# A neighbour mask turned by VectorE instead of TensorE, and the order of the steps around it

## The chip, the cores and the metric

The kernel runs on one core of a Trainium2 chip. The metric is device time in microseconds (us): the median over runs of one whole execution. Below, PE is TensorE's matmul side and PEld its weight loads, DVE is VectorE, ACT is ScalarE, POOL is GpSimd, and SP is the engine on whose queue most DMAs are issued.

## The reference

Two graph layers run over 128 graphs of 128 nodes with 256 channels, in float32. The change lies in the message part of the first layer:

```python
def _L0_gnn_ref(x, mask, w_se, b_se, conv1_w, ..., w_msg, b_msg, w_ih, b_ih, w_hh, b_hh):
    ...                                   # x_conv: two convolutions over the nodes, the second with 17 taps
    s = x @ w_se.T + b_se                 # 3 channels a node
    sq = jnp.sum(s * s, axis=-1)
    dist = sq[:, :, None] + sq[:, None, :] - 2.0 * jnp.einsum('bnd,bmd->bnm', s, s)
    A = jnp.exp(-dist) * mask
    msg = jax.nn.relu(x @ w_msg.T + b_msg)
    x_nmp = jnp.einsum('bnm,bmd->bnd', A, msg)
    x_in = jnp.concatenate([x_conv, x_nmp], axis=-1)
    ...                                   # a GRU cell of x_in and x
    return (1.0 - z) * nn_ + z * x

h = jnp.maximum(_layernorm(x, axis=-1), 0.0)
x = x + _L0_gnn_ref(h, adj, ...)
...                                       # layer 1: five small graph convolutions on the first 25 nodes
```

`adj` is [128, 128, 128] and holds zeros and ones.

## The kernel before

Graphs are worked on in groups of four (`GB`), so there are 32 groups `q`. The program is written as generators, and a small planner decides the order in which their steps are put on the engines' queues.

**The planner.** `Order.run` (lines 183 to 204) takes a set of lanes. A lane holds a list of generators and a weight. Every `yield cost, wait` ends a step: the planner's clock goes on by `cost`, and the generator isn't due again until `wait` later. The planner takes the lane with the least cost done for its weight whose next generator is due. The order is fixed when the program is built; on the chip each engine runs its queue in that order and waits on semaphores.

**The stages.** Lines 1129 to 1150 run two batches, each of a preparing stage and a product stage. `stage_a` (389) normalises 16 groups, transposes them, applies the first convolution and goes to frequencies. `stage_b` (502) does the second convolution as products by frequency: at each of 40 steps it loads weights (`load_w`, 509, `wf`, issued three steps ahead), adds them on POOL (`add`, 517), multiplies on PE (`product`, 523) into PSUM tiles `pa` and `pb`, and evicts with ACT and DVE (556 to 559). A lane called `beside` runs next to all of that: first the weights of the taps, then `early(q)` (662) for q from 0 to 31. After the two batches the gates (`stage_c`, 713), the rest of `beside` and layer 1 share PE (1149).

**The messages of a group.** `early(q)` takes the tiles that were loaded a group ahead, has `load_n(q + 1)` (571) issued on SP's queue, and runs `neighbours` (608). `load_n` loads `hT`, the normalised group with channels on partitions, and `ad`, the mask of four graphs with the target node on partitions. `neighbours` then goes through these steps, with the planner's cost and wait in brackets:

- an embedding on PE into `pse` (614), four scaled copies `ef` on ACT (618) and their product `lr` on DVE (621) [0.5, 0.0];
- twice a message: eight passes on PE into `pm` (630), the bias on DVE (633) and relu on ACT (635) [1.75, 0.0 each];
- the distances: for each of the four graphs a matmul with a 32-row slice of `lr` into the first half of a PSUM tile `pd` (643); for each a transpose of its mask through the identity into the second half (645); for each the exponential on ACT into `aT` (647) and the multiply with the transposed mask, read from PSUM, on DVE (648) [0.9, 3.0];
- twice `px`, the messages times `aT` (656), and its eviction on DVE (658) [0.9, 0.0 each].

PSUM tiles with the tag "tmp" come from one pool of five banks, `ptmp` (218), which all lanes share in turn; the four `pd` tiles take four of them. The SBUF tiles of `neighbours` come from the pool `fr` with one buffer each, those of `load_n` from `io` with two.

These few lines set the step that is changed:

```python
639        pds = [ptmp.tile([P, 2, N], FP, tag="tmp", name=f"pd{q}_{j}") for j in range(GB)]
643            nc.tensor.matmul(pds[j][:, 0], lr[rows, 0], lr[rows, 1], start=True, stop=True)
645            nc.tensor.transpose(pds[j][:, 1], ad[:, j], ident)
647            nc.scalar.activation(aT[:, j], pds[j][:, 0], AF.Exp)
648            nc.vector.tensor_mul(aT[:, j], aT[:, j], pds[j][:, 1])
```

`convolved` (689) has a turn by DVE already: `nc.vector.transpose` (705) turns each 32x32 block of a 128x512 tile by itself. Layer 1 has a load of short runs already, of the first 25 columns of the mask (`prepare`, 964).

Of the kernel before, what the change touches and what calls it, by code (L numbers as in the profile page):

```python
# [9 lines left out]
FP = mybir.dt.float32  # L10
AF = mybir.ActivationFunctionType
# [4 lines left out]
B, N, D = 128, 128, 256  # L16
# [3 lines left out]
P = 128  # L20
GB = 4
# [20 lines left out]
WIDE = 32  # L42
# [165 lines left out]
def kernel(ctx: ExitStack, tc: tile.TileContext, x, adj, consts, vecs, w_se, conv1_w,  # L208
                    conv2_w, w_msg, b_msg, w_ih, w_hh, W1, W2, b2, fusion_w, out):
    nc = tc.nc  # L210
# [7 lines left out]
    ptmp = ctx.enter_context(tc.tile_pool(name="ptmp", bufs=5, space=PSUM))  # L218
# [14 lines left out]
    def c(name):  # L233
        a, b = CAT[name]
        return cst[:, a:b]
# [5 lines left out]
    ident = c("ident")  # L241
# [127 lines left out]
    LATE, XA, MOM = {}, {}, {}  # L369
# [201 lines left out]
    def load_n(q):  # L571
        hT = LATE["io"].tile([P, 2, 512], FP, tag="hT", name=f"hT{q}")
        nc.sync.dma_start(out=hT, in_=hTd[q])
        ad = LATE["io"].tile([P, GB, N], FP, tag="adj", name=f"adj{q}")
        nc.sync.dma_start(out=ad, in_=adj[q * GB:(q + 1) * GB].rearrange("b n m -> n b m"))
        return hT, ad

    SUMS = {}
# [29 lines left out]
    def neighbours(q, hT, ad, xm):  # L608


        pse = ptmp.tile([P, 512], FP, tag="tmp", name=f"pse{q}")
        for k in range(2):
            for j in range(GB):
                nc.tensor.matmul(pse[j * WIDE:(j + 1) * WIDE, :N], wse9[:, k],  # L614
                                 hT[:, k, j * N:(j + 1) * N], start=(k == 0), stop=(k == 1))
        ef = LATE["fr"].tile([P, 4, N], FP, tag="ef", name=f"ef{q}")
        for i in range(4):
            nc.scalar.activation(ef[:, i], pse[:, :N], AF.Identity, scale=emb[:, i:i + 1],
                                 bias=embb[:, i:i + 1])
        lr = LATE["fr"].tile([P, 2, N], FP, tag="lr", name=f"lr{q}")  # L620
        nc.vector.tensor_tensor(lr, ef[:, 0::2], ef[:, 1::2], ALU.mult)
        yield 0.5, 0.0

        msgs = []
        for h in range(2):
            pm = ptmp.tile([P, 2, D], FP, tag="tmp", name=f"pm{q}_{h}")
            for i in range(2):
                j = 2 * h + i
                for k in range(2):
                    nc.tensor.matmul(pm[:, i], hT[:, k, j * N:(j + 1) * N], LATE["wmsg"][:, k],  # L630
                                     start=(k == 0), stop=(k == 1))
            msg = LATE["fr"].tile([P, 2, D], FP, tag=f"msg{h}", name=f"msg{q}_{h}")
            nc.vector.tensor_tensor(
                msg, pm, LATE["bmsg"][:, None, :].to_broadcast([P, 2, D]), ALU.add)
            nc.scalar.activation(msg, msg, AF.Relu)
            msgs.append(msg)
            yield 1.75, 0.0

        pds = [ptmp.tile([P, 2, N], FP, tag="tmp", name=f"pd{q}_{j}") for j in range(GB)]
        aT = LATE["fr"].tile([P, GB, N], FP, tag="aT", name=f"aT{q}")  # L640
        for j in range(GB):
            rows = slice(j * WIDE, (j + 1) * WIDE)
            nc.tensor.matmul(pds[j][:, 0], lr[rows, 0], lr[rows, 1], start=True, stop=True)
        for j in range(GB):
            nc.tensor.transpose(pds[j][:, 1], ad[:, j], ident)
        for j in range(GB):
            nc.scalar.activation(aT[:, j], pds[j][:, 0], AF.Exp)
            nc.vector.tensor_mul(aT[:, j], aT[:, j], pds[j][:, 1])
        yield 0.9, 3.0


        for h in range(2):
            px = ptmp.tile([P, 2, 2, N], FP, tag="tmp", name=f"px{q}_{h}")
            for i in range(2):
                for dc in range(2):
                    nc.tensor.matmul(px[:, dc, i], msgs[h][:, i, dc * P:(dc + 1) * P],  # L656
                                     aT[:, 2 * h + i], start=True, stop=True)
            nc.vector.tensor_copy(xm[:, :, h * 256:(h + 1) * 256],
                                  px.rearrange("p d i n -> p d (i n)"))
            yield 0.9, 0.0  # L660

    def early(q):

        while q not in A_DONE:
            yield 0.0, 0.5
        if q not in EN:
            EN[q] = load_n(q)
            yield 0.0, 6.0
        hT, ad = EN.pop(q)
        if q + 1 < NQ and q + 1 in A_DONE:  # L670
            EN[q + 1] = load_n(q + 1)
        xm = LATE["fr"].tile([P, 2, 512], FP, tag="xnmp", name=f"xnmp{q}", bufs=2)
        yield from neighbours(q, hT, ad, xm)
        nc.gpsimd.dma_start(out=xmd[q], in_=xm)
        E_DONE.add(q)
# [516 lines left out]
```

## Time and profile before

| What | Value |
|---|---|
| median of three runs | 2033.72 us (2030.26 to 2035.86) |
| the profiled run's own time | 2034.12 us |
| span of that run | 2032.3 us |
| TensorE clock granted over the span | 0.994 |
| DMA packets, bytes | 190266, 281.91 MB |
| mask transposes on PE (L645) | 128, 21.0 us busy |
| mask multiplies on DVE (L648) | 128, 28.0 us busy |
| loads of the mask for the messages (L575) | 32 of 256 KB |
| first and last weight load of L645 | 179.1 and 807.5 us |

In rows of instructions the columns are the line, engine, operation, output and inputs, shape and count, then busy us, the mean ns of one, and the idle time of the engine just before them with what ended it. In the order of time a row begins with the start and the length of a run of like instructions, both in us. A busy PE includes the time in which pipelined matmuls drain, so two rows of PE can overlap.

### The profile page before, as it was taken

How to read it: one execution, taken by the hardware profiler on the slowest of the kernel's cores; microseconds unless marked ns; L12 is line 12 of the kernel's file. 1: busy time of each engine (PE TensorE's matmuls, PEld its weight loads, DVE VectorE, ACT ScalarE, POOL GpSimd, SP SyncE). 2: the span in 40 equal slices, each digit the busy share in tenths (PEclk: the TensorE clock that was granted, in tenths of full speed). 3: DMA queues.
4: the chain of work that ended last, by engine and by line, in shares of the span. 5: the costliest groups of instructions: out<-in, count | busy, mean ns of one | idle time of the engine just before them, and what ended most of it. 6: DMA issues, size and time to landing. Idle time of an engine off the chain costs nothing.

```text
span 2032.3 us, 34053 instructions
## 1 busy us (share of the span) xinstructions
PE 1989.3 (98%) x12852; PEld 1653.7 (81%) x12852; DVE 1285.2 (63%) x2807; ACT 683.8 (34%) x1547; POOL 741.2 (36%) x898
## 2 busy tenths in 40 slices
PE   7998999999999999999999999999999999999998
PEld 5666888889888888778788878878888888878875
DVE  6774445785433566766775775677577757766643
ACT  4663222454222344232322322232233322232233
POOL 3542666332655022532333233224323323332330
PEclk9999999999999999999999999999999999999999
DMA  9987879744877633432322322322232323232121
GB/s 214 297 266 226 269 255 285 222 145 161 269 257 254 188 115 89 147 90 68 105 73 84 96 83 73 97 83 80 82 108 68 90 84 93 79 100 84 37 82 53
DMA packets 190266, 281.91 MB, mean 139 GB/s; under 512 B 23745, under 2 KB 143494, under 8 KB 190102
## 3 DMA queue, kind: packets, MB, share of 16 engines
q1 hardware_dynamic: 157062, 185.46, 31.5%
q0 software_dynamic: 32656, 93.98, 14.2%
q8 instruction: 102, 1.67, 0.4%
q14 instruction: 62, 0.51, 0.1%
q10 hardware_dynamic: 384, 0.28, 0.1%
HBM read 187.34 MB, written 92.27 MB: 138 GB/s over the span
## 4 chain that ended last, share of the span: by engine, by line
PE 90%; DVE 3%; issue 2%; DMA 2%; POOL 2%; ACT 1%; SPq 0%; POOLq 0%; DVEq 0%; ACTq 0%
PE p L741 41%; PE pa L526 7%; PE pm L630 5%; PE ph L1049 5%; PE pz L1058 5%; PE pc L421 4%; PE pb L526 3%; PE px L656 3%; PE pf L432 3%; PE pi L698 3%; PE po L887 1%; PE ph L410 1%; PE py L1032 1%; PE pw L474 1%; PE pse L614 1%
## 5 line engine op out<-in xcount | busy, mean ns | idle before, releaser
L867 POOL TENSOR_TENSOR hTc<-hTc,r 128x512 f32<-128x512 f32 x64 | 88.7, 1385 | 255.8 <-ACT r L864 255.8
L526 PE MATMUL pa<-wf,X 128*128 128x256 f32 x640 | 152.2, 381 | 0.0
L558 DVE SCALAR_TENSOR_TENSOR y<-pa,kk 128x512 f32<-128x512 f32 x78 | 53.8, 690 | 151.2 <-ACT kk L557 151.1
L896 POOL DMA_DIRECT2D out<-xt x128 | 72.0, 569 | 175.1 <-DVE xt L893 172.0
L741 PE MATMUL p<-th,wrz 128*128 128x256 f32 x512 | 134.6, 385 | 0.0
L741 PE MATMUL p<-tc,wrz 128*128 128x256 f32 x512 | 131.5, 379 | 0.0
L741 PE MATMUL p<-tm,wrz 128*128 128x256 f32 x512 | 131.4, 379 | 0.0
L526 PEld LDWEIGHTS pa<-wf,X 128*128 128x128 f32 x640 | 118.2, 190 | 16.1 <-issue 2.0
L421 PE MATMUL pc<-c1w,hTa 128*128 128x256 f32 x512 | 122.3, 386 | 1.9 <-DVE X L438 1.7
L630 PE MATMUL pm<-wmsg,hT 128*128 128x256 f32 x512 | 123.4, 387 | 0.0
L1051 ACT ACTIVATE hh<-ph,vec 128x96 f32<-128x96 f32 (+3 forms) x160 | 63.8, 401 | 140.8 <-PE ph L1049 131.7
L1049 PE MATMUL ph<-yz,w 128*128 128x96 f32 (+3 forms) x640 | 109.7, 325 | 1.0 <-issue 1.0
L421 PEld LDWEIGHTS pc<-c1w,hTa 128*128 128x128 f32 x512 | 95.0, 192 | 18.9 <-DVE h L424 4.8
L741 PEld LDWEIGHTS p<-th,wrz 128*128 128x128 f32 x512 | 94.6, 190 | 19.1 <-issue 7.4
L630 PEld LDWEIGHTS pm<-wmsg,hT 128*128 128x128 f32 x512 | 97.0, 193 | 16.1 <-issue 1.6
L710 ACT ACTIVATE xc<-xc,t_bn 128x256 f32<-128x256 f32 x128 | 58.0, 500 | 149.2 <-DVE xc L707 149.2
L741 PEld LDWEIGHTS p<-tm,wrz 128*128 128x128 f32 x512 | 97.4, 190 | 13.1
L1058 PE MATMUL pz<-hh,w 128*128 128x96 f32 (+3 forms) x640 | 107.3, 322 | 0.0
L1049 PEld LDWEIGHTS ph<-yz,w 128*128 128x128 f32 x640 | 88.4, 194 | 21.3 <-issue 14.5
L741 PEld LDWEIGHTS p<-tc,wrz 128*128 128x128 f32 x512 | 95.0, 190 | 11.6
L1058 PEld LDWEIGHTS pz<-hh,w 128*128 128x128 f32 x640 | 86.6, 191 | 17.7
L741 PE MATMUL p<-hTc,wrz 128*128 128x256 f32 x384 | 98.9, 380 | 0.0
(200 smaller groups left out, 4579.5 us busy)
## 6 DMA issues: line engine op xcount, KB each, us to landing
wf<-wfd SPq DMA_DIRECT2D x160, 256.0 KB
wfd<-ws POOLq DMA_DIRECT2D x64, 320.0 KB, 9.2
yd<-y POOLq DMA_DIRECT2D x80, 256.0 KB, 4.1
yt<-yd SPq DMA_DIRECT2D x64, 320.0 KB
w<-in_W SPq DMA_DIRECT2D x40, 512.0 KB
xa<-in_x SPq DMA_DIRECT2D x128, 128.0 KB
hTd<-hTa POOLq DMA_DIRECT2D x32, 512.0 KB, 6.5
hT<-hTd SPq DMA_DIRECT2D x32, 512.0 KB
```

The costliest lines, as they stand in the source:

```text
L421: nc.tensor.matmul(pc[:, i], hT[:, k, (2 * h + i) * N:(2 * h + i + 1) * N], c1w[:, k], start=(k == 0), stop=(k == 1))
L432: nc.tensor.matmul(pf[:, i, :F * NB], h1[:, 2 * h + i, k * P:(k + 1) * P], fwd, start=True, stop=True)
L526: nc.tensor.matmul(ps, xk(k), WF[f][:, k, s], start=(k == 0), stop=(k == 1))
L630: nc.tensor.matmul(pm[:, i], hT[:, k, j * N:(j + 1) * N], LATE["wmsg"][:, k], start=(k == 0), stop=(k == 1))
L656: nc.tensor.matmul(px[:, dc, i], msgs[h][:, i, dc * P:(dc + 1) * P], aT[:, 2 * h + i], start=True, stop=True)
L698: nc.tensor.matmul(pi[w * WIDE:(w + 1) * WIDE, :, :, n].rearrange("p k g c -> p g k c"), inv[:F, o:o + WIDE], yt[:, n // 2::2].rearrange(" ...
L741: nc.tensor.matmul(ps[:, m], w[:, i, k, m * P:(m + 1) * P], factor(i, x, t), start=first and j == 0, stop=last and j == len(n) - 1, skip_g ...
L867: nc.gpsimd.tensor_sub(d, d, r[:, dc])
L896: nc.gpsimd.dma_start(out=out[q * GB + j, WIDE:].rearrange("(t n) c -> n t c", n=WIDE), in_=xt[j * WIDE:(j + 1) * WIDE, 1:4])
L1049: nc.tensor.matmul(ph, w1[:, k, m * P:(m + 1) * P], yz[:, k, :, o:o + n], start=(k == 0), stop=(k == 1))
L1051: nc.scalar.activation(hh[:, m], ph, AF.Relu, bias=v("b1", g * 4 + m))
L1058: nc.tensor.matmul(pz, w2[:, g, m, cc * P:(cc + 1) * P], hs[g][:, m], start=(m == 0), stop=(m == 3))
```

## The change

The mask is loaded in blocks: four DMAs a group, one for each 32 columns, put each 32x32 block of a mask where one turn by DVE of the 128x512 tile gives the transposed mask `adT` in SBUF. The runs in memory become 32 elements (128 bytes) long instead of 128. The four transposes on PE are gone, and so is the second half of each `pd`. The turn is the first instruction of `neighbours`. The multiplies read two SBUF tiles, and there are two of 128x256 instead of four of 128x128. The distances move between the first and the second message, and the costs and waits that the steps tell the planner change from (0.5, 0), (1.75, 0), (1.75, 0), (0.9, 3.0) to (0.5, 0), (1.75, 3.0), (0.45, 3.0), (1.75, 0.3); the two of `px` stay.

```diff
     def load_n(q):
...
-        ad = LATE["io"].tile([P, GB, N], FP, tag="adj", name=f"adj{q}")
-        nc.sync.dma_start(out=ad, in_=adj[q * GB:(q + 1) * GB].rearrange("b n m -> n b m"))
+        ad = LATE["io"].tile([P, GB * 4, WIDE], FP, tag="adj", name=f"adj{q}")
+        for w in range(4):
+            nc.sync.dma_start(out=ad[w * WIDE:(w + 1) * WIDE],
+                              in_=adj[q * GB:(q + 1) * GB, :, w * WIDE:(w + 1) * WIDE]
+                              .rearrange("b (k n) m -> n (b k) m", n=WIDE))
...
     def neighbours(q, hT, ad, xm):
+        adT = LATE["fr"].tile([P, GB, N], FP, tag="adT", name=f"adT{q}")
+        nc.vector.transpose(adT.rearrange("p b n -> p (b n)"),
+                            ad.rearrange("p b n -> p (b n)"))
         pse = ptmp.tile([P, 512], FP, tag="tmp", name=f"pse{q}")
...
-        for h in range(2):
+        def message(h):
             pm = ptmp.tile([P, 2, D], FP, tag="tmp", name=f"pm{q}_{h}")
...
-            yield 1.75, 0.0
-        pds = [ptmp.tile([P, 2, N], FP, tag="tmp", name=f"pd{q}_{j}") for j in range(GB)]
+        message(0)
+        yield 1.75, 3.0
+        pds = [ptmp.tile([P, N], FP, tag="tmp", name=f"pd{q}_{j}") for j in range(GB)]
         aT = LATE["fr"].tile([P, GB, N], FP, tag="aT", name=f"aT{q}")
         for j in range(GB):
             rows = slice(j * WIDE, (j + 1) * WIDE)
-            nc.tensor.matmul(pds[j][:, 0], lr[rows, 0], lr[rows, 1], start=True, stop=True)
+            nc.tensor.matmul(pds[j], lr[rows, 0], lr[rows, 1], start=True, stop=True)
         for j in range(GB):
-            nc.tensor.transpose(pds[j][:, 1], ad[:, j], ident)
-        for j in range(GB):
-            nc.scalar.activation(aT[:, j], pds[j][:, 0], AF.Exp)
-            nc.vector.tensor_mul(aT[:, j], aT[:, j], pds[j][:, 1])
-        yield 0.9, 3.0
+            nc.scalar.activation(aT[:, j], pds[j], AF.Exp)
+            if j % 2:
+                nc.vector.tensor_mul(aT[:, j - 1:j + 1], aT[:, j - 1:j + 1], adT[:, j - 1:j + 1])
+        yield 0.45, 3.0
+        message(1)
+        yield 1.75, 0.3
```

## The prediction

> **What bounds the kernel now.** I read the page's busy shares first, then a table of stretches, then the order of instructions around one mask, then who waits for whom.
>
> ```profile
> PE 1989.3 (98%) x12852; PEld 1653.7 (81%) x12852; DVE 1285.2 (63%) x2807; ACT 683.8 (34%) x1547; POOL 741.2 (36%) x898
> ...
> PE 90%; DVE 3%; issue 2%; DMA 2%; POOL 2%; ACT 1%; SPq 0%; POOLq 0%; DVEq 0%; ACTq 0%
> ```
>
> TensorE is busy for 98% of the span and makes 90% of the chain that ended last. A busy PE includes pipelined ends, so the price of an instruction has to come from the distance to the next start, not from its duration.
>
> ```profile
> 280.00:490.00 210.00, 206.37 (x1315) 183.31 (x1314) 141.23 (x351) 86.65 (x207) 90.93 (x110) 1.00 0.65 205
> 490.00:560.00 70.00, 70.00 (x437) 60.98 (x436) 29.95 (x55) 21.98 (x57) 38.92 (x48) 1.00 0.80 266
> 560.00:690.00 130.00, 128.82 (x877) 109.38 (x876) 56.08 (x119) 41.29 (x115) 64.38 (x82) 1.00 0.77 251
> 690.00:820.00 130.00, 128.59 (x909) 109.83 (x908) 86.41 (x175) 54.37 (x111) 27.46 (x29) 1.00 0.38 108
> ```
>
> Columns: stretch in us, its length, then busy us of PE, PEld, DVE, ACT, POOL, the granted clock, the DMA share, GB/s. All 32 groups of messages run from 168 to 813 us. By the starts of their loads, 3 stand before the first frequency products, 8 beside them (196 to 345), 5 beside the second preparing stage, 10 beside the second products (508 to 668) and 6 beside the gates. PE has next to no idle time in these rows; DVE is at 67% and 66% in the first and last of them, and the DMA engines at 0.80 and 0.77 beside the products. The granted clock is 1.00, so no throttle hides a saving.
>
> **The price of what is removed.** Four mask transposes leave PE in each group.
>
> ```profile
> 520.91 0.31 PEld L643 LDWEIGHTS pd<-lr 32*128 32x128 f32 x8 [0.33 <-issue]
> 521.35 0.42 PEld L645 LDWEIGHTS pd<-cst,adj 128*128 128x128 f32 x4
> 521.73 1.60 PEld L526 LDWEIGHTS pa<-wf,X 128*128 128x128 f32 x8
> ```
>
> The four begin at 521.35 and the next work begins loading at 521.73, although each matmul is reported at 273 ns. Their room is 0.38 us; in ten groups I read 0.38 or 0.39 (once 0.58, with a wait in it). 32 x 0.388 = 12.4 us. The page's 21.0 us of busy time for L645 would overstate it. The step back from 32-row weights (0.13 us from 521.22 to 521.35) stays, since some full-size work follows anyway. I take -12.4 us; nothing covers these transposes, because PE has other lanes' work ready right behind them.
>
> [...]
>
> **Waits on PE that belong to the mask.**
>
> ```profile
> PE px L656 <- DVE aT L648: 2.3, 3, 1.0
> ...
> PE ph L410 <- DVE aT L648: 0.9, 1, 0.9
> ...
> PE pf L432 <- DVE aT L648: 0.8, 2, 0.5
> ```
>
> Today the multiply reads PSUM, so it is what frees four of the five shared banks; other lanes' work (ph, pf, and 0.2 us of pi) waits for it. After the change the exponential frees the bank. That takes away 0.9 + 0.8 + 0.2 = 1.9 us; the 2.3 us of px may go too, since a message now stands between exponentials and px. Bounds -4.2 to 0; I take -1.9.
>
> **What DVE takes over.**
>
> ```profile
> L705 DVE STREAM_TRANSPOSE xc<-pi 128x512 f32<-128x512 f32 x64 | 45.6, 712 | 2.6 <-PE pi L698 0.8
> ...
> L621 DVE TENSOR_TENSOR lr<-ef x32: 416/426/3476, 175.0 to 801.0; 128x256 f32<-128x256 f32 x32
> L586 DVE TENSOR_TENSOR tc<-tc,xc x32: 419/1483/1491, 690.2 to 1917.4; 128x256 f32<-128x256 f32 x32
> ```
>
> One turn of 128x512 costs about 0.71 us by L705, which has the same shape and the same operation from PSUM; from SBUF it isn't in the trace, and I keep the value. The four multiplies of a group take 0.88 us together (the x4 rows at 180.35, 190.25 and 788.90); two of 128x256 with both inputs in SBUF take 2 x 0.43 = 0.85 by the median of L621, or 2 x 1.48 = 2.97 by the median of L586's tc, which is long where POOL is at work. So DVE gains 0.7 to 2.8 us a group. Beside the products DVE is at 43%, and this lies beside other work. In the preparing stage and beside the gates (5 + 6 = 11 groups, DVE at two thirds) late evictions could hold PE: from 0 to 11 x 2.8 = 31 us. PE waits in the whole of 690 to 820 only 1.4 us, so there is slack of that order in its buffers; I take +1.5. The turn stands at the head of `neighbours` and waits for four loads; queued behind it on DVE are lr, the messages' additions and the other lane's evictions. For 31 groups the loads were issued one group ahead (17 us or more). For the first they follow the hT load for which PE waits 7.8 us at 172.3, so lr there may come up to 3 us late. I take +0.5.
>
> **Spacing.** lr is now needed after one message, not two. In the first group pse began at 172.31 and lr ended at 175.45, 3.1 us later; pse and one message fill 0.6 + 1.7 to 2.0 us. Without another lane's step between, PE would wait about 0.5 us. The planner's new due time (3.0 after the first message, 3.0 after the distances) lets in one step of 2.6 of the products or of 0.9 to 2.6 of the others, so I charge it only to the first three groups, which run almost alone, less the 1.0 us that px waits there today: +0.5, bounds 0 to 16 (32 x 0.5). The second message's relu is needed after px of the first half; its due time of 0.3 again lets another lane in. The planner sees 6.25 instead of 6.7 units a group, so a group more may fall beside the products; that moves work, and PE is full in both places.
>
> **Loads.** Each mask becomes 2048 runs of 128 B in four loads instead of 512 of 512 B in one. The nearest row is the layer-1 mask's load (100 B runs), which stood alone on the queues from 842.5 to 843.5:
>
> ```profile
> DMA packets 302, 0.03 MB, mean 29 GB/s; under 512 B 302, under 2 KB 302, under 8 KB 302
> ...
> q1 hardware_dynamic: 302, 0.03, 23.8%
> ```
>
> 0.238 x 16 us / 302 = 12.6 ns a packet. The old mask's load, from 774.4 to 775.2:
>
> ```profile
> DMA packets 401, 0.23 MB, mean 291 GB/s; under 512 B 16, under 2 KB 391, under 8 KB 401
> ...
> q1 hardware_dynamic: 401, 0.23, 92.6%
> ```
>
> 0.926 x 16 x 0.8 = 11.9 us over 375 runs of 512 B, 31 ns at most. Each of 16 engines thus carries 32 x 31 = 1.0 us before, and 128 x 12.6 = 1.6 us after, or 128 x 31 = 4.0 us if a short run costs what a long one does. Beside the second products a group comes every 17.4 us and leaves 0.23 x 17.4 = 4.0 us of the engines free; the added 0.6 to 3.0 us fits. I take 0. The three further issues on SP (0.43 us each, 1.3 a group) stand ahead of the wf loads, which are issued three steps (some 12 us) before use; covered, and if that cover went, 1.3 us in 18 groups would be 23 us.
>
> [...]
>
> **Sum.** -12.4 - 1.9 + 1.5 + 0.5 + 0.5 + 0 = -11.8 us. The profiled run took 2034.1, which gives 2022.3. The median shown is 0.4 lower, so **2022 us**. Its own range, from the bounds of the small terms: 2014 to 2027.
>
> **Rivals.**
> - *The cover is lost* (chance 0.17, no measurable change). If no other lane's step falls between first message and distances, 0.5 us in 32 groups: 2034.1 - 12.4 - 1.9 + 16 = 2036. For it: 0.33 us of waiting stands ahead of L643 already, even with two messages as cover. Against it: the due times.
> - *DVE becomes the bound* (0.10, slower). In the preparing stage and beside the gates the turn and the blocked multiplies delay evictions, and PE waits. It decides for slower from (12.4 + 6.1) / 11 = 1.7 us of PE's time a group. Between that and 2.8, 2.25 x 11 = 25 us: 2034.1 - 12.4 + 25 = 2047. For it: tc's 1483 ns. Against it: at these multiplies' times in the timeline DVE often idles for the exponential.
> - *Short runs fill the DMA engines* (0.07, slower). It decides from a packet price at which 128 x price - 1.0 exceeds 4.0, that is 39 ns. The dearest nearby row is that of the x loads, also into 32 partitions: 206 packets at 111.4% from 749.5 to 750.5, 86 ns for 1 KB. Half-way between 31 and 86, 58 ns: (7.4 - 1.0 - 4.0) x 18 groups = 43 us, 2034.1 - 12.4 + 43 = 2065. Against it: the 12.6 ns.
>
> **How the numbers follow.** 0.66 for the forecast, 0.17, 0.10 and 0.07 for the rivals. About 0.3% (6.1 us) is what a measurement of this kernel can tell from no change. Faster 0.66, same 0.17, slower 0.17. The range reaches from the forecast's low end to where the lost cover and the mild end of the DVE rival lie: 2014 to 2042.
>
> **What would show it.** Right: no transposes of the mask on PE; the distances followed by other work at once; 32 turns of about 0.71 us on DVE, not waiting for a DMA after the first; PE idle between 170 and 820 no larger than now; wf loads never waited for. Wrong: PE waiting at the distances for lr (cover), at evictions by DVE around 345 to 490 and 690 to 820 with multiplies over 1 us (DVE), or a DMA share near 1 beside the products with PE waiting for wf.

## The result, and the profile after

The changed kernel takes 2044.69 us (median of ten runs, 2037.72 to 2048.28) where the kernel before takes 2034.65 beside it. The ratio is 1.0052, with a 95% interval of 1.0037 to 1.0067: 0.5% slower, where 2022 us was forecast. Below, ratios are turned into microseconds of this 2034.65, so the change is +10.6 us (7.5 to 13.6); a ratio is not the quotient of the two medians and can differ from it by some 0.2%. The profiled run took 2043.16 us with a span of 2041.4 and a mean granted clock of 0.989 (before: 2034.12, 2032.3, 0.994).

From the page after, the busy shares and the shares of the chain that ended last:

```profile
PE 1986.4 (97%) x12724; PEld 1645.0 (81%) x12724; DVE 1300.7 (64%) x2775; ACT 677.3 (33%) x1543; POOL 738.2 (36%) x898
...
PE 88%; issue 3%; DVE 3%; DMA 2%; POOL 2%; ACT 1%; SPq 0%; DVEq 0%; POOLq 0%; ACTq 0%
```

The 128 transposes are gone from PE (12852 - 12724). Its busy time fell by only 2.9 us while the span grew by 9.1, so PE now idles more, and part of what it does it does more slowly. Both are seen in stretches of 20 us. First after, then before, then e1_old_steps (the changed kernel with its steps in the old order, below); the columns are the stretch, its length, busy us of PE, PEld, DVE, ACT and POOL, the granted clock, the DMA share and GB/s.

```profile
420.00:440.00 20.00, 16.27 (x81) 13.73 (x80) 13.58 (x28) 8.61 (x20) 6.74 (x7) 0.83 0.30 98
500.00:520.00 20.00, 18.36 (x112) 15.83 (x111) 9.91 (x12) 6.21 (x18) 7.32 (x9) 0.91 0.63 183
680.00:700.00 20.00, 11.93 (x124) 9.87 (x126) 9.40 (x20) 5.05 (x16) 1.08 (x2) 0.86 0.72 218
700.00:720.00 20.00, 20.00 (x154) 16.84 (x147) 9.43 (x21) 6.35 (x12) 0.00 (x0) 0.88 0.17 46
```

```profile
420.00:440.00 20.00, 20.00 (x135) 18.22 (x134) 15.52 (x40) 10.72 (x22) 9.63 (x12) 1.00 0.64 209
500.00:520.00 20.00, 20.00 (x122) 17.17 (x121) 8.38 (x16) 5.83 (x15) 10.74 (x14) 1.00 0.66 226
680.00:700.00 20.00, 19.79 (x195) 16.69 (x197) 11.43 (x28) 8.00 (x19) 0.54 (x1) 1.00 0.52 134
```

```profile
420.00:440.00 20.00, 20.00 (x137) 18.37 (x136) 17.38 (x45) 10.44 (x23) 5.98 (x9) 1.00 0.60 195
500.00:520.00 20.00, 20.00 (x124) 17.21 (x123) 9.21 (x14) 5.44 (x15) 12.32 (x16) 1.00 0.86 265
680.00:700.00 20.00, 20.00 (x149) 17.38 (x149) 12.03 (x26) 7.07 (x15) 0.00 (x0) 1.00 0.52 108
```

Four of the stretches that carry it are shown: a place inside the second preparing stage (420), the start of the second products (500), and the start of the gates (680 and 700). In the first three PE runs dry, and in all four the clock falls. Before and e1 hold 1.00 in all four; the longest idle time there is 1.2 us, in e1 from 700 to 720. Summed over the 35 such stretches from 160 to 860 us, PE idles 32.8 us after and 17.6 before (e1: 22.3), and the length times (1 - clock) is 17.4 us after and 3.4 before (e1: 8.8). These two add to +29.2 us, somewhat too much since a low clock during an idle time is counted twice. Less 12.4 for the transposes and 6.1 for the same two sums ahead of 160 us (17.7 before, 11.6 after), and with 1.2 behind 860, that gives about +12 against the 9.1 of the spans.

Whom PE waited for after, with the total, how often, and the longest, in us:

```profile
PE pse L620 <- DMA hT<-hTd: 10.7, 1, 10.7
PE pi L706 <- DMA yt<-yd: 7.1, 1, 7.1
PE pc L421 <- DVE h L424: 3.5, 3, 2.9
...
PE pd L651 <- DVE lr L627: 2.3, 3, 1.6
PE pa L526 <- DMA wf<-wfd: 2.3, 1, 2.3
```

The waits of `ph` and `pf` for `aT` that were shown before are gone, as forecast. In their place stand `pi` waiting for `yt`, `pd` waiting for `lr`, and `pc` waiting for an eviction. The first row is not new in kind: `hT` lands at 172.3 us in both kernels, and PE only comes to it earlier.

**The start of the gates.** The order on PE after, with the idle time ahead of an instruction in brackets:

```profile
687.32 1.99 PE L637 MATMUL pm<-wmsg,hT 128*128 128x256 f32 x8
689.63 0.58 PE L651 MATMUL pd<-lr 32*128 32x128 f32 x8 [0.32 <-DVE lr L627]
697.30 3.64 PE L706 MATMUL pi<-yt,cst 80*32 80x128 f32 x64 [7.10 <-DMA yt<-yd]
700.88 2.08 PE L749 MATMUL p<-hTc,wrz 128*128 128x256 f32 x4
```

Behind the distances PE's queue has `convolved`, not the second message, which the planner holds for 3.0, and the input of `convolved` had only just been asked for. The hold alone doesn't explain it: in e4, below, the second message stands there, and PE still waits 4.1 us for `yt`. SP's queue at that time, each row with its start and its length:

```profile
684.24 0.32 SPq L573 DMA_DIRECT2D hT<-hTd  x1
684.61 2.59 SPq L576 DMA_DIRECT2D adj<-in_adj  x4
687.25 2.67 SPq L689 DMA_DIRECT2D hTc<-hTd  x1
689.97 0.46 SPq L691 DMA_DIRECT2D xm<-xmd  x1
690.47 0.94 SPq L608 DMA_DIRECT2D yt<-yd  x2
```

`yt` is issued at 690.47, behind four mask loads that take 2.59 us and a load of `hTc`; PE then stands for 7.10 us. The same place in the kernel before, on PE and, in the second fence, on SP:

```profile
678.90 0.65 PE L614 MATMUL pse<-hT,wse 128*32 128x128 f32 x16
679.48 3.72 PE L630 MATMUL pm<-wmsg,hT 128*128 128x256 f32 x16
683.13 0.50 PE L643 MATMUL pd<-lr 32*128 32x128 f32 x8
683.56 0.66 PE L645 MATMUL pd<-cst,adj 128*128 128x128 f32 x4
684.15 1.08 PE L698 MATMUL pi<-yt,cst 80*32 80x128 f32 x32
```

```profile
671.96 1.37 SPq L605 DMA_DIRECT2D yt<-yd  x2
```

There `yt` was asked for 12 us before its use, and the messages of two groups (from 671.2 and 679.5) stood between. What follows the gap in the changed kernel is shown by finer stretches:

```profile
694.00:696.00 2.00, 0.00 (x0) 0.00 (x0) 0.76 (x2) 0.40 (x3) 0.00 (x0) 0.62 1.08 302
696.00:700.00 4.00, 2.70 (x52) 2.73 (x56) 0.70 (x1) 0.00 (x0) 0.00 (x0) 0.50 0.39 76
700.00:704.00 4.00, 4.00 (x27) 3.02 (x20) 3.57 (x9) 1.81 (x4) 0.00 (x0) 0.50 0.59 164
704.00:708.00 4.00, 4.00 (x18) 3.50 (x17) 0.44 (x2) 0.60 (x1) 0.00 (x0) 0.91 0.00 0
```

The clock falls to 0.50 while PE stands, at about 694.5, and stays there until about 704.7, so `pi` and the first `p` run at half clock: 3.64 and 2.08 us, against 1.95 and 1.13 in e5 (below), where the clock is 1.00 at their place.

**The start of the second products.** `lr` is one multiply of 128x256 on DVE with both factors in SBUF, ahead of the distances. On DVE, POOL and PE after:

```profile
508.80 3.47 DVE L627 TENSOR_TENSOR lr<-ef 128x256 f32<-128x256 f32 x1 [0.89 <-ACT ef L624]
```

```profile
508.13 0.74 POOL L520 TENSOR_TENSOR xs<-X 128x256 f32<-128x256 f32 x1
508.82 1.27 POOL L521 TENSOR_TENSOR wf<-wf 128x512 f32<-128x512 f32 x1
510.04 0.73 POOL L520 TENSOR_TENSOR xs<-X 128x256 f32<-128x256 f32 x1
510.72 1.26 POOL L521 TENSOR_TENSOR wf<-wf 128x512 f32<-128x512 f32 x1
```

```profile
512.42 0.58 PE L651 MATMUL pd<-lr 32*128 32x128 f32 x8 [1.64 <-DVE lr L627]
```

`lr` starts at 508.80 and ends just after POOL's four additions, at about 512; its median is 0.43. The four of the 32 that took over 1 us (1.64 to 3.47) lie beside POOL's additions, and the other 28 took 0.38 to 0.43. In the kernel before, twelve of the 32 took 0.6 to 3.5 us, and PE waited for none, with two messages ahead of the distances. With one, PE waits 1.64 us here. Then the clock falls: 0.90, 0.50 and 0.75 in the three stretches of 2 us from 512 to 518.

**The preparing stage** (420 to 434), on PE and on DVE after:

```profile
422.31 0.97 PE L651 MATMUL pd<-lr 32*128 32x128 f32 x4 [0.72 <-ACT hTa L412]
426.20 6.40 PE L421 MATMUL pc<-c1w,hTa 128*128 128x256 f32 x16 [2.92 <-DVE h L424]
```

```profile
421.01 4.54 DVE L278 TENSOR_SCALAR xa<-xa,mv,rs 128x256 f32<-128x256 f32 x4
```

`pd` waits 0.72 us for a bank, and then `pc` 2.92 us for the eviction of `h`, which stands on DVE behind four normalising instructions of 4.54 us together. POOL works at the same time, and that this is what makes them long was not tested. Before, `px` and transforms of other groups fill PE there. The clock from 420 to 440 is 0.83.

### The profile page after: what moved, and what is told of

It is laid out like the page before. It is cut to its first block, busy times and chain, and to the rows that moved or that the text cites. A ratio compares the mean times of both kernels' runs of the same rounds, so it can differ in the third digit from the quotient of the medians.

```text
span 2041.4 us, 33977 instructions
## 1 busy us (share of the span) xinstructions
PE 1986.4 (97%) x12724; PEld 1645.0 (81%) x12724; DVE 1300.7 (64%) x2775; ACT 677.3 (33%) x1543; POOL 738.2 (36%) x898
## 4 chain that ended last, share of the span: by engine, by line
PE 88%; issue 3%; DVE 3%; DMA 2%; POOL 2%; ACT 1%; SPq 0%; DVEq 0%; POOLq 0%; ACTq 0%
PE p L749 39%; PE pa L526 7%; PE pm L637 5%; PE ph L1057 5%; PE pz L1066 5%; PE pc L421 5%; PE pb L526 3%; PE pf L432 3%; PE pi L706 3%; PE px L664 3%; PE pw L474 2%; PE ph L410 1%; PE po L895 1%; PE py L1040 1%; DMA wfd<-ws 1%
## 5 line engine op out<-in xcount | busy, mean ns | idle before, releaser
L749 PEld LDWEIGHTS p<-tc,wrz 128*128 128x128 f32 x512 | 94.9, 190 | 11.6
L521 POOL TENSOR_TENSOR wf<-wf 128x512 f32<-128x512 f32 x78 | 98.5, 1262 | 5.7 <-DMA wf<-wfd 5.7
```

Source lines behind the costliest of these rows:

```text
L521: nc.gpsimd.tensor_tensor(WF[f][:, :, 2], WF[f][:, :, 0], WF[f][:, :, 1], ALU.add)
L749: nc.tensor.matmul(ps[:, m], w[:, i, k, m * P:(m + 1) * P], factor(i, x, t), start=first and j == 0, stop=last and j == len(n) - 1, skip_g ...
```

## The experiments

Each kernel was timed in five rounds beside the kernel before. All diffs are against the changed kernel unless said.

**Which part costs: the engines or the order?** e1_old_steps keeps the loads, the turn and the multiplies, and puts the old order of the steps back:

```diff
         message(0)
-        yield 1.75, 3.0
+        yield 1.75, 0.0
+        message(1)
+        yield 1.75, 0.0
         pds = [ptmp.tile([P, N], FP, tag="tmp", name=f"pd{q}_{j}") for j in range(GB)]
...
-        yield 0.45, 3.0
-        message(1)
-        yield 1.75, 0.3
+        yield 0.9, 3.0
```

> Turn by VectorE, short-run loads and the multiplies from SBUF as in the change; steps in the old order (both messages, then the distances) with the planner's old costs and waits, so that PE's order is that of the kernel before without the 128 transposes. Theory S (the new steps open gaps at the ends of the stages, where PE waits and its clock falls): the 12.4 us of the transposes come out, 2022 us (ratio to before 0.994), granted clock back at about 0.994, no wait of 7 us at pi. Theory L (the short runs hold up SP's queue and the DMA engines): 2040 or more, a ratio of 1.003 or more, with PE still waiting on loads. Theory V (the turn and the multiplies on VectorE delay evictions): the same 2040 or more, with PE waiting on VectorE between 345 and 500 us.

Measured: 2030.14 us, ratio 0.9961 (0.9948 to 0.9975), -7.9 us; by the medians (2034.41 before) it is -4.3. e2_spacing_only is the other half, the kernel before with the new order and waits alone (diff against before):

```diff
-        for h in range(2):
+        def message(h):
...
-            yield 1.75, 0.0
+        message(0)
+        yield 1.75, 3.0
         pds = [ptmp.tile([P, 2, N], FP, tag="tmp", name=f"pd{q}_{j}") for j in range(GB)]
...
-        yield 0.9, 3.0
+        yield 0.45, 3.0
+        message(1)
+        yield 1.75, 0.3
```

> The kernel before with its loads, PE transposes and PSUM multiplies, and only the steps changed: distances between the messages, with the new costs and waits. Theory S: slower by what the change lost in gaps and clock, some 20 us: 2050 to 2058 us (ratio about 1.01), granted clock 0.987 to 0.989. Theories L and V: 2034, a ratio of 1.000 within 0.003.

Measured: 2046.43 us, 1.0059 (1.0040 to 1.0077), +12.0 us. The waits of e2 name the same places as those of the changed kernel, with no turn and no short runs in it:

```profile
PE pi L701 <- DMA yt<-yd: 5.5, 1, 5.5
PE pd L644 <- DVE lr L621: 2.3, 3, 1.6
```

So the order loses more than the engines gain. The halves don't simply add: -7.9 and +12.0 make +4.1, and the whole is +10.6. With the turn by DVE the new steps cost 18.5 us (1.0052 against e1's 0.9961), without it 12.0. The 6.5 us between lie at the edge of what these runs resolve, and where they arise is not shown.

**Order or waits?** e4_order_no_wait keeps the new place of the distances and moves the one long wait to the end, where it was before; e7_waits_old_place has the long waits and the old place (diff against e1).

```diff
-        yield 1.75, 3.0
+        yield 1.75, 0.0
...
-        yield 0.45, 3.0
+        yield 0.45, 0.0
         message(1)
-        yield 1.75, 0.3
+        yield 1.75, 3.0
```

> The change with the distances between the messages, but the planner's waits moved: 0 after the first message and after the distances, 3.0 after the second message. The four steps before px then go back to back. Theory S in the form that the waits are to blame: 2022 to 2028. Theory S in the form that the place of the distances is to blame (lr is due one message earlier): PE waits at the distances for lr, and the time stays at 2034 or more. L and V: 2044.

```diff
-        yield 1.75, 0.0
+        yield 1.75, 3.0
         message(1)
-        yield 1.75, 0.0
+        yield 1.75, 3.0
...
-        yield 0.9, 3.0
+        yield 0.45, 0.3
```

> The kernel with the turn by VectorE in the old order (both messages, then the distances), with the new wide waits: 3.0 after each message, 0.3 after the distances. If the waits are what opens the gaps: no faster than 2040, with PE idle at about 690 us and a granted clock of 0.989 or less. If the place of the distances is what does it: 2030, as with the old steps.

| ratio to before, with the turn by DVE | old place | new place |
|---|---|---|
| waits as before | 0.9961 (e1) | 1.0076 (e4: 1.0058 to 1.0095) |
| new waits | 0.9992 (e7: 0.9978 to 1.0006) | 1.0052 (the change) |

e7's 2033.33 us lies between the two outcomes that were named. The place of the distances costs 23 us without the new waits and 12 with them. The new waits cost 6.3 us in the old place, where they open the gap at the start of the gates too (e7's stretch from 680 to 700 has PE busy for 12.93 us at a clock of 0.66); in the new place they may save a little, but those two intervals overlap. e4's rows for `lr` and for who waited show why the new place needs cover:

```profile
L627 DVE TENSOR_TENSOR lr<-ef x32: 384/2334/3468, 174.2 to 746.4; 128x256 f32<-128x256 f32 x32
```

```profile
PE pd L651 <- DVE lr L627: 7.2, 4, 3.4
```

The three durations are shortest, median and longest in ns. With the steps close together the median of `lr` is 2.33 us, against 0.43 in the changed kernel, and PE waits 7.2 us for it in four groups.

**Is it the two factors in SBUF?** e10_no_wait_lr_psum is e4 with the odd factors of `lr` written by ACT into the free part of `pse`, in PSUM, so that DVE reads one factor from SBUF (diff against e4):

```diff
-        ef = LATE["fr"].tile([P, 4, N], FP, tag="ef", name=f"ef{q}")
+        ef = LATE["fr"].tile([P, 2, N], FP, tag="ef", name=f"ef{q}")
+        eo = pse[:, N:3 * N].rearrange("p (i n) -> p i n", i=2)
         for i in range(4):
-            nc.scalar.activation(ef[:, i], pse[:, :N], AF.Identity, scale=emb[:, i:i + 1],
-                                 bias=embb[:, i:i + 1])
+            nc.scalar.activation((eo if i % 2 else ef)[:, i // 2], pse[:, :N], AF.Identity,
+                                 scale=emb[:, i:i + 1], bias=embb[:, i:i + 1])
         lr = LATE["fr"].tile([P, 2, N], FP, tag="lr", name=f"lr{q}")
-        nc.vector.tensor_tensor(lr, ef[:, 0::2], ef[:, 1::2], ALU.mult)
+        nc.vector.tensor_tensor(lr, ef, eo, ALU.mult)
```

> The kernel with the new order and no waits between (2053 us), with one factor of lr written to PSUM by ACT, so that lr's multiply reads one SBUF and one PSUM tile instead of two SBUF tiles. Theory P (lr is late because its multiply is held for 3.4 us while POOL adds at the start of the products and beside them, and the new order needs it one message earlier): lr takes 0.45 us at most everywhere, the wait of the distances for lr falls from 7.2 us to under 2, and the time by 6 to 10 us, to about 2045. Rival Q (lr is late because of the queue on ACT and VectorE ahead of it): lr's longest time falls but the wait stays over 5 us and the time within 3 us of 2053.

Measured: 2037.86 us, 1.0015 (0.9997 to 1.0034), 12 us less than e4 by the ratios and 9.3 by the spans (2043.5 and 2034.2).

```profile
L628 DVE TENSOR_TENSOR lr<-ef,pse x32: 383/422/423, 173.5 to 735.9; 128x256 f32<-128x256 f32 x32
```

Not one of the 32 is long any more, and PE's wait for `lr` falls from 7.2 to 1.2 us. With two factors in SBUF `lr` took up to 3.47 us (e4), with one in PSUM 0.42 at the most (e10). What passes between DVE and POOL while it is long, the runs don't show.

**The start of the gates.** e5_keep_busy puts 14 unused products into the gap ahead of the first `convolved`; e11_yt_first issues the two `yt` loads of the first group before the gates' lanes begin.

```diff
             yield 0.0, 6.0
+            keep = ptmp.tile([P, 512], FP, tag="tmp", name="keep")
+            for _ in range(14):
+                nc.tensor.matmul(keep[:, :D], ident, LATE["wrz"][:, 0, 0], start=True, stop=True)
```

> The change, with 14 matmuls of 256 columns (some 6 us, their result unused) put on PE ahead of the first inverse transform, where PE waits 7.1 us for yt at about 690 us; the planner's costs are untouched, so the order is the same. Theory K (an idle gap of PE costs twice: the wait itself, and half clock for some 8 us after it): the wait at pi shrinks to 1 to 2 us, the clock stays at 1.00 between 680 and 720 us, and the kernel is 4 to 6 us faster than the change, about 2039, although it does more work. Without K (the gap is the whole price): 2044, or 1 us more.

Measured: 2045.45 us, 1.0051 (1.0035 to 1.0067), no change. PE in e5:

```profile
690.33 0.58 PE L651 MATMUL pd<-lr 32*128 32x128 f32 x8 [0.31 <-DVE lr L627]
693.77 8.00 PE L733 MATMUL keep<-wrz,cst 128*128 128x256 f32 x28 [2.86 <-DVE msg L640]
701.70 1.95 PE L706 MATMUL pi<-yt,cst 80*32 80x128 f32 x64
...
706.28 1.03 PE L752 MATMUL p<-th,wrz 128*128 128x256 f32 x4
```

The filling itself waited 2.86 us for a bank, and the clock fell behind that wait:

```profile
694.00:696.00 2.00, 2.00 (x7) 1.66 (x7) 0.76 (x2) 1.10 (x5) 0.00 (x0) 0.66 1.03 372
696.00:698.00 2.00, 2.00 (x6) 1.55 (x6) 0.00 (x0) 0.00 (x0) 0.00 (x0) 0.50 1.09 214
```

From 698 on it was back at 0.99 to 1.00, so here it is the filling that ran slowly, and `pi` began at a clock of 1.00: from `pi` to the first `p` of `th` PE takes 4.58 us (701.70 to 706.28), against 8.16 in the changed kernel (697.30 to 705.46). So the half clock behind the gap is worth 3.6 us. Nothing was gained, because the filling ended late: counted from `pd`, `th` begins after 15.95 us, and after 15.83 in the changed kernel. The size of the price is shown; this filling is no remedy.

```diff
         if q == 0:
-            load_yt(q, 0)
-            load_yt(q, 1)
             yield 0.0, 6.0
...
         tc.tile_pool(name="co", bufs=1, side="right", reuse_waits="tile"))
+    load_yt(0, 0)
+    load_yt(0, 1)
```

> The change with the first group's two yt loads issued as the first loads of the gates' stage, ahead of hTc, xm, the next hT and the four mask loads. Theory S (the step order leaves too little work on PE for the loads to hide behind; 7.1 us of waiting there and 5 us of clock): the wait at pi falls to under 2 us, the clock stays at 1.00 from 690 to 710 us, and the time falls by 8 to 12 us, to about 2034. If PE then waits for hTc or xm instead, by 3 us or less. If the gap isn't what costs: 2044.

Measured: 2041.15 us, 1.0035 (1.0017 to 1.0054), 3.5 us less, and not told apart from the change by the intervals. PE and DVE in e11:

```profile
695.94 3.64 PE L706 MATMUL pi<-yt,cst 80*32 80x128 f32 x64 [3.48 <-DVE msg L640]
```

```profile
694.87 0.42 DVE L589 TENSOR_TENSOR tm<-tm,xm 128x256 f32<-128x256 f32 x1
695.21 0.68 DVE L640 TENSOR_TENSOR msg<-pm,bmsg 128x512 f32<-128x512 f32 x1
```

`yt` is in time, and another wait takes its place: `pi` needs a bank that the message's addition frees, and that addition stands on DVE behind eight subtractions of the gates (L589, from 692.27). PE stands for 3.48 us instead of 7.10, and `pi` still takes 3.64 us, at a clock of 0.50 (from 696 to 704). The forecast of 8 to 12 us for this edit was too high. e12_yt_first_lr_psum has e11's edit and e10's:

> Both edits on the change. Theories S and P together: 2034 less the gap at 512 us (1.6 us of waiting for lr and 1.8 us of clock), 2029 to 2032, no wait of the distances for lr over 0.4 us, granted clock 0.991 or more. What stays is the gap at 420 us (3.7 us and 3.4 us of clock), where VectorE's normalising was held for 4.5 us.

Measured: 2035.60 us, 1.0013 (0.9997 to 1.0030), 7.9 us less than the change by the ratios. The two remedies bring the new order back to the time before, though not to e1's, nor to the 2029 to 2032 that was expected: `pi` still waits 3.3 us for the message's addition.

**The loads and the turn.** e3_long_runs loads the mask as before, with one DMA of long runs; e9_old_steps_long_runs is the same in the old order; e8_no_turn is e9 with `adT = ad`. In e3 and e9 the mask is turned only within its 32x32 blocks, and e8 leaves the turn out.

```diff
-        ad = LATE["io"].tile([P, GB * 4, WIDE], FP, tag="adj", name=f"adj{q}")
-        for w in range(4):
-            nc.sync.dma_start(out=ad[w * WIDE:(w + 1) * WIDE],
-                              in_=adj[q * GB:(q + 1) * GB, :, w * WIDE:(w + 1) * WIDE]
-                              .rearrange("b (k n) m -> n (b k) m", n=WIDE))
+        ad = LATE["io"].tile([P, GB, N], FP, tag="adj", name=f"adj{q}")
+        nc.sync.dma_start(out=ad, in_=adj[q * GB:(q + 1) * GB].rearrange("b n m -> n b m"))
```

> The change with the mask loaded as before, one DMA of 512 B runs a group; the turn by VectorE then transposes each 32x32 block in place, so the mask that multiplies is only turned within blocks. Theory L: back to 2022, or at least 10 us faster than the change, and the wait for yt at about 690 us is gone. Theory S: within 5 us of the change's 2044, since the gaps come from the order. Theory V: 2044.

> Old steps, turn by VectorE, one load of long runs a group (the turn then works within 32x32 blocks in place, so the mask is only turned within blocks). Theory L, in the size that the change without short runs showed (4 us): 2026. If the short runs cost only where the loads of the products queue behind them at a stage's start: 2028 to 2030.

> Old steps, one load of long runs a group, and no turn at all: the multiplies take the mask as it was loaded (the masks here are symmetric, so the turn is left out). It bounds what the turn and the short runs cost where the order is good. If they cost nothing (as predicted): 2030, as with the old steps. If the missing 4 us of the expected 12.4 lie in them: 2022 to 2026.

Measured: e3 2040.08 us, 1.0031 (1.0018 to 1.0045); e9 2028.53, 0.9965 (0.9952 to 0.9979); e8 2023.51, 0.9945 (0.9929 to 0.9962). Short runs cost 4 us in the new order, with intervals that overlap, and nothing that can be told in the old (e1 0.9961, e9 0.9965). The turn may cost 4 us (e9 against e8); those intervals overlap too, so this stays open. With neither, the removal of the transposes, with the banks that it frees, is worth -11.2 us (-14.4 to -7.7).

**The best of both.** e13_old_steps_lr_psum is e1 with e10's edit of `lr`.

> The fastest version so far (old steps, turn by VectorE) with lr's factor in PSUM. In the old order two messages cover lr, so P expects nothing at the distances: within 3 us of 2030; a little less VectorE time (lr's held multiplies). Faster by over 4 us would mean that lr's held multiply delays other evictions too.

Measured: 2024.81 us, 0.9960 (0.9942 to 0.9977), -8.1 us. By the ratio it is e1's equal: where two messages cover `lr`, its length costs nothing that these runs resolve. By the medians it is 5 us faster than e1, each taken beside much the same time before (2034.08 and 2034.41), so a small gain from other evictions isn't ruled out. e1 and e13 are both faster than the kernel before and than the change.

## Why the forecast was wrong, step by step

- **The transposes** (-12.4): right, within what the runs resolve. e8 has -11.2, with the freed banks in it; e1, with the turn and the short runs, -7.9. The 4 us that e1 lacks against 12.4 fit the turn or PE's 4.8 us of waiting for `aT` at `px` (three times), but e8 has that wait too; they are not settled.
- **The waits for banks** (-1.9): right for `ph` and `pf`, which the list after doesn't show. What that is worth by itself no run separates.
- **The turn and the multiplies** (+1.5): the sizes were right; what they cost PE stays open, 0 to 4 us by e8 and e9. The turn was costed from the one that reads PSUM, and measured:

```profile
L615 DVE STREAM_TRANSPOSE adT<-adj x32: 700/702/711, 173.8 to 784.3; 128x512 f32<-128x512 f32 x32
```

  DVE stood idle ahead of it for its loads only in the first group, 11.4 us, and `lr` there ended no later than before (both began at 175.0).
- **The loads** (0): nearly right for the DMA engines. Their share from 540 to 660 us rose from 0.77 to 0.87, and PE waited for `wf` once, 2.3 us at 189 us, behind the mask loads. What was too low is the issue on SP: 2.0 to 2.7 us for the four in 27 of the 32 groups and 4.65 at the most, not 1.7, and in one place they stand ahead of `yt`. e2 waits 5.5 us for `yt` with a single mask load there, so they aren't needed for that gap. In the new order e3 puts the short runs at 4 us, which isn't told apart from nothing.
- **Spacing** (+0.5, bounds 0 to 16): this is the step that failed. It priced one thing, `lr` due after one message, at 0.5 us in three groups, and trusted the due times for the rest. e2 measures the step by itself: +12.0 us (8.1 to 15.7), and beside the turn it costs 18.5. That 12.0 lies within the bounds is luck: they stand for 0.5 us of waiting for `lr` in each of 32 groups, and in e2 and in the changed kernel that wait comes to 2.3 us in three. Three things stood in its place. First, the price of a late `lr` was taken from the first group, where it took 0.43 us, as it does by the median; the same row, quoted in the forecast, had 3476 ns as its longest, and that is what the distances met (1.64 us of waiting at 510, up to 3.4 in e4). Secondly, a step that isn't due is not only room for another lane's step but also work that is missing where no other lane has any: at the start of the gates and in the preparing stage. The forecast looked at the 32 groups as alike and not at the stages' ends. Thirdly, it said that "the granted clock is 1.00, so no throttle hides a saving". That was true of the kernel before, and says nothing of a kernel with longer gaps: the length times (1 - clock) went from 3.4 to 17.4 us.
- **The rivals**: "the cover is lost" came nearest, but it named one of the three places and the smallest, the distances (2.3 us of waiting for `lr`), and got 2036 us by spreading 0.5 us over 32 groups. The wait for `yt` at the gates, that for `h` in the preparing stage and the slow clock behind each are not in it. The 0.33 us ahead of L643 that it counted for itself is put down in its row to "issue" on PEld, not to `lr`. DVE did not become the bound (64% busy), and the DMA engines did not fill (0.87 from 540 to 660 us).
- **The range**: 2014 to 2027 doesn't follow from the bounds that are given for the small terms. Only that of the waits for banks reaches below zero, which leads to 2034.1 - 12.4 - 4.2 = 2017.5, and the upper bound of spacing alone adds 16.

Not settled: why the wait of 1.64 us at 510 takes the clock down in the changed kernel (0.91 from 500 to 520) and not in e2 and e11 (1.00 in theirs, with PE busy for the same 18.36 us); why the place of the distances costs 23 us without the waits, of which `lr` explains some 12 (e10); and where the 6.5 us arise by which the whole exceeds its halves.

## What to carry to other kernels

When a step is moved or held back, ask at each stage's beginning and end what PE has left to do, and price a gap as its length plus what a lower clock behind it costs (here 3.6 us behind 7.10), not by an average over all groups. Take the longest duration of a row, not its median, for an operation that comes onto the path, and look at what the other engines were doing when it was long. When a change has an engine part and an order part, run each by itself: here one is worth -7.9 us and the other +12.0. And time the whole as well: it is +10.6, not their sum.

## What the runs showed of the hardware

- A gap of 7.10 us on PE cost 3.6 us more in the work behind it, with a granted clock of 0.50 from about 694.5 to 704.7 us, the last 7.4 us of it under work (the changed kernel; the price from e5 against it).
- Half clock was also seen behind waits of 2.86 us (0.50 from 696 to 698 us in e5) and of only 1.64 us (0.50 from 514 to 516 us in the changed kernel). In e2, where PE was busy for the same 18.36 us from 500 to 520, the clock was 1.00 there.
- `lr`, a DVE multiply with two factors in SBUF, took 3.47 us beside four POOL additions, 8 times its median of 0.43 (the changed kernel); with one factor in PSUM the longest of 32 took 0.42 us (e10).
